# Seven block products for eight in the first product of a stacked graph network's layer 0

## The chip, the cores and the metric

The kernel runs on one core of a Trainium2 chip. The metric is device time in microseconds (us). The core works through its engines, each with its own queue of instructions: TensorE (PE in the profile) multiplies matrices, its weight loads are listed apart (PEld); VectorE (DVE), ScalarE (ACT) and GpSimd (POOL) work elementwise; SyncE (SP) issues most transfers. Before the change the kernel takes 2193.2 us, the median of three runs (2192.66 to 2193.32).

## The reference

Four graph layers are stacked over 128 graphs of 64 nodes with 256 features, all in float32, each followed by `x = layernorm(x + layer(x))`. Layer 0 is five small two-layer graph convolutions over groups of the first 25 nodes, weighted and summed:

```python
GROUPS = [list(range(25)), [0, 1, ..., 8], [0, 9, ..., 14], [6, 7, 8, 12, 13, 14], [3, 4, 5, 9, 10, 11]]

def _graph_conv(x, adj, W, b):
    A = adj + jnp.eye(n)
    ...                                  # dinv = rowsum(A) ** -0.5
    norm_adj = dinv[:, :, None] * A * dinv[:, None, :]
    support = jnp.einsum('bnd,de->bne', x, W)
    return relu(jnp.einsum('bnm,bme->bne', norm_adj, support) + b)

for g, idx in enumerate(GROUPS):
    h = _graph_conv(x[:, idx], adj[:, idx][:, :, idx], W1[g], b1[g])      # 256 -> 512
    out_g = _graph_conv(h, adj[:, idx][:, :, idx], W2[g], b2[g])          # 512 -> 256
    fused = fused.at[:, idx].add(softmax(fusion_w)[g] * out_g)
```

Layer 1 is a graph convolution over all 64 nodes, layer 2 a polynomial graph filter, and layer 3 five rounds of message passing with a GRU cell (products with `weight[l]`, `w_ih` and `w_hh`, of 256 and 768 outputs). Layer 3 is most of the work.

## The kernel before

Layer 0 goes through 16 units, numbered from 0. A unit takes up to four tiles of graphs of one group, and its columns are nodes. Groups come in the order 1, 2, 3, 4, 0, so units 0 to 2 belong to group 1 (504, 504 and 144 columns), 3 and 4 to group 2 (448 each), 5 and 6 to group 3 (504, 264), 7 and 8 to group 4 (504, 264), and 9 to 15 to group 0 (500 each, the last 200). For each unit the kernel gathers with the normalised adjacency (`aggregate`), multiplies by W1 (`hidden`), multiplies by W2 (`support`), gathers again (`add`) and, in group 0, normalises (`finish`):

```python
W1 = w0.tile([128, NG, 2, HID], F32, name="W1")      # all five groups' weights stay
W2 = w0.tile([128, NG, 4, D], F32, name="W2")
...
def aggregate(i):
    ...
    for k in range(2):
        p = psum0("pa0")
        for t, r in enumerate(u.rows):
            nc.tensor.matmul(p[:, u.off[t] : u.off[t] + r], xg[:r, t, k * 128 : (k + 1) * 128], AT[:r, t, :r], ...)
        with tc.high_priority():
            nc.scalar.copy(ag0[:, k, : u.cols], p[:, : u.cols])

def hidden(i):
    u = UNITS[i]
    ag0 = AG.pop(i)
    hg = keep.tile([128, 4, 512], F32, tag="NI", name="hg", bufs=2)
    for e in range(4):
        p = psum0("ph")[:, : u.cols]
        for k in range(2):
            nc.tensor.matmul(
                p, W1[:, u.g, k, e * 128 : (e + 1) * 128], ag0[:, k, : u.cols], start=k == 0, stop=k == 1
            )
        relus.append(
            nc.scalar.activation(hg[:, e, : u.cols], p, AF.Relu, bias=b1[:, u.g * 4 + e : u.g * 4 + e + 1])
        )
    HG[i] = hg

def support(i):
    ...
    for v in range(0, len(u.tiles), 2):
        p = psum0("ps").rearrange("p (t d) -> p t d", t=2)
        ts = range(v, min(v + 2, len(u.tiles)))
        for t in ts:
            for e in range(4):
                nc.tensor.matmul(
                    p[: u.rows[t], t - v, :], hg[:, e, u.off[t] : u.off[t] + u.rows[t]], W2[:, u.g, e, :],
                    start=e == 0, stop=e == 3,
                )
        ...                                          # copied to s2 on ScalarE
```

`prep` loads and normalises a unit's adjacency on DVE and POOL and transposes it on TensorE. The stages of neighbouring units are interleaved, and the order in which TensorE takes them is the order of this loop:

```python
for i in range(-2, NU + 1):
    if i >= 0:
        stage(load0, i + 3)
    stage(add, i - 1)
    if i:
        stage(aggregate, i + 1)
    early_stage(i, 0)
    stage(support, i)
    ...
    stage(finish, i - 1, g0)
    early_stage(i, 1)
    if i == -1:
        hidden(0)
        ...
    else:
        stage(prep, i + 2)
        stage(hidden, i + 1)
    if i == -2:
        load0(1, powers[0])
        load_second(1)
        load0(2, powers[0])
        load_first(2)
    elif i == -1:
        load_second(2)
        load_first(3)
    elif i == 0:
        load_second(3)
    elif i < 5:
        (load_first, load_second)[(i - 1) % 2]((4, 0)[(i - 1) // 2])
    early_stage(i, 2)
    for f, j in ((store_others, i - 1), (others, i), (load_others, i + 2)):
        ...            # the nodes outside the groups: load, layernorm, store
```

`load_first(g)` and `load_second(g)` load W1 and W2 of a group, each in one transfer of 512 KB. After layer 0 a `fold` multiplies the message weights of layer 3 with `w_ih`. Layer 3's products are already made by seven block products for eight: with both factors cut into 2x2 blocks, seven products of blocks and sums of blocks, added up rightly, give what eight block products give. The sums of weight blocks are `factors` (on DVE), those of data blocks `sums` (on POOL), and the additions of the products lie in the class `Gates` (copies on ACT, additions on DVE).

Of the kernel before, what the change touches and what calls it, by code (L numbers as in the profile page):

```python
# [68 lines left out]
def gnn_stack(  # L69
# [118 lines left out]

    def load_adj(c):
        a64 = keep.tile([128, NP, N], F32, name="a64", bufs=2)  # L190
        nc.sync.dma_start(a64, av[c])
        adjs[c] = a64
# [142 lines left out]
    with ExitStack() as c0:  # L335
        w0 = c0.enter_context(tc.tile_pool(name="w0", bufs=1))
        work = c0.enter_context(tc.tile_pool(name="work0", bufs=1))
        W1 = w0.tile([128, NG, 2, HID], F32, name="W1")
        W2 = w0.tile([128, NG, 4, D], F32, name="W2")
# [3 lines left out]
        loads, A, AG, HG, S2, Z, XO = {}, {}, {}, {}, {}, {}, {}  # L343
# [77 lines left out]
        def hidden(i):  # L421
            u = UNITS[i]
            ag0 = AG.pop(i)
            hg = keep.tile([128, 4, 512], F32, tag="NI", name="hg", bufs=2)
            for e in range(4):
                p = psum0("ph")[:, : u.cols]
                for k in range(2):
                    nc.tensor.matmul(  # L428
                        p, W1[:, u.g, k, e * 128 : (e + 1) * 128], ag0[:, k, : u.cols], start=k == 0, stop=k == 1
                    )  # L430
                relus.append(
                    nc.scalar.activation(hg[:, e, : u.cols], p, AF.Relu, bias=b1[:, u.g * 4 + e : u.g * 4 + e + 1])
                )
            HG[i] = hg

        def support(i):
            u = UNITS[i]
            hg, s2 = HG.pop(i), []
            for v in range(0, len(u.tiles), 2):
                p = psum0("ps").rearrange("p (t d) -> p t d", t=2)  # L440
                ts = range(v, min(v + 2, len(u.tiles)))
                for t in ts:
                    for e in range(4):
                        nc.tensor.matmul(  # L444
                            p[: u.rows[t], t - v, :], hg[:, e, u.off[t] : u.off[t] + u.rows[t]], W2[:, u.g, e, :],
                            start=e == 0, stop=e == 3,
                        )
                sv = work.tile([TR, 2, D], F32, name="s2", bufs=4)
                if u.rows[ts[0]] == u.rows[ts[-1]]:
                    nc.scalar.copy(sv[: u.rows[v], : len(ts), :], p[: u.rows[v], : len(ts), :])  # L450
                else:
                    for t in ts:
                        nc.scalar.copy(sv[: u.rows[t], t - v, :], p[: u.rows[t], t - v, :])
                s2 += [sv[:, t - v, :] for t in ts]
            S2[i] = s2
# [66 lines left out]
        def others(i):  # L522

            with tc.issue_after(evictions[-1].ins):
                layernorm(XO[i], n=XO[i].shape[1])

        def store_others(i):
            t = XO.pop(i)
            nc.sync.dma_start(xb[:, NP * i : NP * i + t.shape[1], :], t)
# [19 lines left out]
        def load_first(g):  # L549
            nc.sync.dma_start(W1[:, g], w1[g].rearrange("(k p) e -> p k e", p=128))  # L550

        def load_second(g):
            nc.sync.dma_start(W2[:, g], w2[g].rearrange("(k p) e -> p k e", p=128))

# [25 lines left out]
        g0 = next(i for i, u in enumerate(UNITS) if u.g == 0)  # L580
        for i in range(-2, NU + 1):
            if i >= 0:
                stage(load0, i + 3)
            stage(add, i - 1)
            if i:
                stage(aggregate, i + 1)
            early_stage(i, 0)
            stage(support, i)
            if not i:
                aggregate(1)  # L590
            if i == NU:
                folds = [products(0, q) for q in range(3)]
            stage(finish, i - 1, g0)
            early_stage(i, 1)
            if i == -1:

                hidden(0)
                with tc.issue_after(evictions[0].ins):
                    prep(1)
            else:  # L600
                stage(prep, i + 2)
                stage(hidden, i + 1)
            if i == -2:
                load0(1, powers[0])
                load_second(1)
                load0(2, powers[0])
                load_first(2)
            elif i == -1:
                load_second(2)
                load_first(3)  # L610
            elif i == 0:
                load_second(3)
            elif i < 5:
                (load_first, load_second)[(i - 1) % 2]((4, 0)[(i - 1) // 2])
# [58 lines left out]

# [4 lines left out]

    def factors(w):

        nc.vector.tensor_sub(w[:, :, 5, :], w[:, :, 4, :], w[:, :, 0, :])
        nc.vector.tensor_sub(w[:, :, 2, :], w[:, :, 1, :], w[:, :, 5, :])

    def fold():
# [7 lines left out]
        for l in range(L):  # L692
            for q in range(3):
# [10 lines left out]
                if q == 2:  # L704
                    factors(V[l])
                if q == 2 and l == 0:
                    nc.vector.tensor_add(WHH[:, :, 4, :], w21, WHH[:, :, 3, :])
                    nc.vector.tensor_sub(WHH[:, :, 6, :], WHH[:, :, 0, :], w21)
                    factors(WHH)
                yield  # L710

    def sums(a, name):

        t = work.tile([128, 4, H], F32, tag="T" + name, name="T" + name, bufs=2)
        nc.gpsimd.tensor_sub(t[:, 0:2, :], a[:, :, H:], a[:, 0, :].rearrange("p (s n) -> p s n", s=2))  # L715
        nc.gpsimd.tensor_sub(t[:, 2, :], a[:, 1, H:], t[:, 0, :])
        nc.gpsimd.tensor_sub(t[:, 3, :], a[:, 1, :H], t[:, 2, :])
        return t

    class Gates:  # L720

        def __init__(self, C, sides, name):
            self.C, self.sides, self.name = C, sides, name
            self.copies = {}

        def multiply(self, bank, i):
            for g, side in enumerate(self.sides):
                for m, (w, q, a, t) in enumerate(side):  # L730
                    rhs = {
                        1: a[:, 0, :H], 2: a[:, 1, :H], 3: a[:, 1, H:], 4: t[:, 3, :], 5: t[:, 0, :], 6: t[:, 2, :],
                        7: t[:, 1, :],
                    }[i]
                    nc.tensor.matmul(  # L735
                        bank[:, g, :], w[:, q, i - 1, :], rhs, start=i in (1, 2, 5) and g == 0 and m == 0,
                        stop=m == len(side) - 1, skip_group_check=True,
                    )

        def bank(self, s):  # L740
            return pg.tile([128, 2, H], F32, tag="pg", name=f"p{s}{self.name}")

        def product(self, i):
            C = self.C
            if i == 1:
                self.a = self.bank("a")
            if i in (1, 6, 7, 4):
                self.multiply(self.a, i)
                if i != 4:
                    c = self.copies[i] = work.tile([128, 2, H], F32, tag="copy", name=f"c{i}", bufs=4)  # L750
                    with tc.high_priority():
                        nc.scalar.copy(c, self.a)  # L752
                if i == 7:
                    nc.vector.tensor_add(C[:, :, 1, H:], self.d, self.copies.pop(7))  # L754
            elif i == 2:
                b = self.bank("b")
                self.multiply(b, i)
                nc.vector.tensor_add(C[:, :, 0, :H], b, self.copies.pop(1))  # L758
            else:
                if i == 5:  # L760
                    self.d = self.bank("d")
                self.multiply(self.d, i)
                if i == 3:
                    nc.vector.tensor_add(C[:, :, 0, H:], self.d, self.copies.pop(6))  # L764

    class Chunk:
# [12 lines left out]
        def state_of_layer2(self, k):  # L779
            if k:  # L780
                self.hT = work.tile([128, 2, NP * 128], F32, tag="hT", name="hT", bufs=4)
            p = self.transpose(lambda q, k: self.xt[:, q, k * 128 : (k + 1) * 128], k, "pT3")
            nc.scalar.copy(self.hT[:, k, :], p)
            if not k:
                self.th = sums(self.hT, "h")

        def messages(self, h=None):
            self.agg = gather(self.xt if h is None else h, self.A01, "agg", work, "agg", 2)
            self.ta = sums(self.agg, "a")

        def rz(self, i):
            if i == 1:
                self.RZ = keep.tile([128, 2, 2, NP * 128], F32, tag="RZ", name="RZ", bufs=2)
                self.g = Gates(
                    self.RZ, [[(WHH, q, self.hT, self.th), (V[self.l], q, self.agg, self.ta)] for q in (0, 1)], "rz"
                )
            self.g.product(i)
            RZ = self.RZ
            if self.last:
                self.last_rz(i)  # L800
                return
            for q in range(2):
# [8 lines left out]
        def n(self, i):  # L811
            if i == 1:
                self.NI = keep.tile([128, 2, 2, NP * 128], F32, tag="NI", name="NI", bufs=2)
                self.gn = Gates(
                    self.NI, [[(V[self.l], 2, self.agg, self.ta)], [(WHH, 2, self.hT, self.th)]], "n"
# [91 lines left out]
        def turn(self, k):  # L907
# [9 lines left out]
            if not last:  # L917
                with tc.high_priority():
                    nc.scalar.copy(self.h[:, :, f], pv)
                if not k:  # L920
                    self.th = sums(self.hT, "h")
# [175 lines left out]
```

## Time and profile before

| | before |
|---|---|
| median of three runs | 2193.2 us |
| profiled run | 2192.7 us |
| TensorE clock granted | 0.998 |
| ACT copies of layer 3's seven-product scheme, 128x512 (`c` L752) | 586 ns each |
| POOL 128x512 subtraction (`Ta` L715) | 1277 ns each |
| layer 0, fold, layer 3 | to 295 us, to 328 us, to the end |

The profile counts a float32 matmul as two records, so a group marked x16 is eight matmuls. A name such as `L428` is a line of the kernel: L428 is the matmul of `hidden`, L444 that of `support`, L413 and L466 those of `aggregate` and `add`, L399 the transposes of `prep`. A line of a timeline gives start and duration of a group of like instructions; because a group's last instruction overlaps the next group's first, the time that a group takes on TensorE is read from its start to the start of the next. A line of the waits gives total, number and longest wait in us. A line of groups gives busy time and mean length in ns, and then the idle time before it with what ended it.

### The profile page before, as it was taken

The page shows a single profiled execution, that of the slowest core. Times are in us where ns is not written, and L with a number is a line of the kernel's source. Part 1 is how long each engine was busy: PE and PEld are TensorE (multiplying, and loading weights), DVE is VectorE, ACT ScalarE, POOL GpSimd, SP SyncE. Part 2 cuts the span into 40 slices and gives each one's busy share as a digit, 9 for nine tenths or more (in the row PEclk, how much of TensorE's full clock was granted, in tenths as well). Part 3 has the DMA queues.
Part 4 walks back from the last instruction along what each step waited for, and adds up shares of the span by engine and source line. Part 5 has one row for each costly group of instructions (what it writes and reads, how often), then busy time and mean ns, then how long its engine had stood idle before and what let it go on. Part 6 is the DMA issues. An engine that isn't in the chain of part 4 may idle for free.

```text
span 2190.9 us, 30164 instructions
## 1 busy us (share of the span) xinstructions
PE 2176.9 (99%) x11542; PEld 1907.6 (87%) x11542; DVE 1363.6 (62%) x3067; ACT 1004.1 (46%) x1845; POOL 572.4 (26%) x621
## 2 busy tenths in 40 slices
PE   9999999999999999999999999999999999999998
PEld 6777888898988889888889898889898898888887
DVE  3445666566766666666766666657656666566556
ACT  3333334544544554444444454445444544455454
POOL 3211131222332222222322232232322222232222
PEclk9999999999999999999999999999999999999999
DMA  6532110000100010000000010001000000000000
GB/s 165 177 124 66 49 37 3 1 3 1 42 1 3 1 39 4 3 1 20 22 3 1 1 42 1 3 1 42 1 1 1 20 10 1 1 10 11 1 1 20
DMA packets 54204, 51.12 MB, mean 23 GB/s; under 512 B 20910, under 2 KB 49068, under 8 KB 54060
## 3 DMA queue, kind: packets, MB, share of 16 engines
q1 hardware_dynamic: 49552, 43.83, 6.6%
q0 software_dynamic: 1936, 4.83, 0.8%
q8 instruction: 91, 1.49, 0.3%
q10 hardware_dynamic: 2572, 0.54, 0.1%
q14 instruction: 53, 0.43, 0.1%
HBM read 32.40 MB, written 16.78 MB: 22 GB/s over the span
## 4 chain that ended last, share of the span: by engine, by line
PE 97%; DVE 2%; POOL 0%; issue 0%; ACT 0%; DMA 0%; ACTq 0%; POOLq 0%; DVEq 0%
PE parz L735 25%; PE pan L735 12%; PE pdrz L735 12%; PE pa L210 9%; PE pbrz L735 6%; PE pdn L735 6%; PE ps L444 4%; PE ph L428 4%; PE pT L776 4%; PE pbn L735 3%; PE pd L288 3%; PE pd L309 2%; PE pa L413 1%; PE po L466 1%; PE pf L562 1%; PE pp L278 1%
## 5 line engine op out<-in xcount | busy, mean ns | idle before, releaser
L752 ACT COPY c<-parz 128x512 f32<-128x512 f32 x240 | 140.7, 586 | 319.8 <-PE parz L735 319.2
L735 PE MATMUL parz<-Th,WHH 128*128 128x256 f32 x960 | 285.9, 379 | 0.2 <-ACT c L752 0.2
L735 PE MATMUL parz<-Ta,V 128*128 128x256 f32 x960 | 285.5, 379 | 0.0
L715 POOL TENSOR_TENSOR Th<-hn 128x512 f32<-128x512 f32 x64 | 81.6, 1275 | 777.6 <-DVE hn L840 602.9
L752 ACT COPY c<-pan 128x512 f32<-128x512 f32 x237 | 139.2, 587 | 149.5 <-PE pan L735 149.4
L837 ACT ACTIVATE NI<-NI,bih 128x512 f32<-128x512 f32 x158 | 113.9, 721 | 201.7 <-DVE NI L832 201.6
L735 PEld LDWEIGHTS parz<-Ta,V 128*128 128x128 f32 x960 | 182.4, 190 | 24.8
L735 PEld LDWEIGHTS parz<-Th,WHH 128*128 128x128 f32 x960 | 176.2, 190 | 21.3 <-ACT c L752 0.7
L809 ACT ACTIVATE RZ<-RZ,brz 128x512 f32<-128x512 f32 x158 | 114.6, 726 | 136.8 <-DVE RZ L764 136.8
L715 POOL TENSOR_TENSOR Ta<-agg 128x512 f32<-128x512 f32 x80 | 102.2, 1277 | 260.4 <-ACT agg L214 260.4
L764 DVE TENSOR_TENSOR RZ<-pdrz,c 128x512 f32<-128x512 f32 x80 | 55.0, 688 | 173.2 <-PE pdrz L735 173.2
L735 PE MATMUL pan<-Ta,V 128*128 128x256 f32 x474 | 141.2, 380 | 0.0
L735 PE MATMUL pan<-Th,WHH 128*128 128x256 f32 x474 | 141.0, 379 | 0.0
L139 POOL TENSOR_TENSOR rs<-ve,mhalf 128x4 f32<-128x4 f32 (+2 forms) x65 | 67.3, 1036 | 281.9 <-DVE ve L137 221.4
L758 DVE TENSOR_TENSOR NI<-pbn,c 128x512 f32<-128x512 f32 x79 | 54.7, 692 | 127.3 <-PE pbn L735 110.1
L210 PEld LDWEIGHTS pa<-A,h 128*128 128x128 f32 x1024 | 124.4, 192 | 3.3
L754 DVE TENSOR_TENSOR NI<-pdn,c 128x512 f32<-128x512 f32 x79 | 54.5, 690 | 112.8 <-ACT c L752 112.8
L210 PE MATMUL pa<-A,h 128*128 128x128 f32 x1024 | 124.6, 275 | 0.0
L838 DVE TENSOR_TENSOR RZ<-hn,NI 128x512 f32<-128x512 f32 x126 | 86.5, 687 | 48.5 <-ACT NI L837 48.5
L840 DVE TENSOR_TENSOR hn<-RZ,NI 128x512 f32<-128x512 f32 x158 | 108.4, 686 | 1.8
L839 DVE TENSOR_TENSOR RZ<-RZ 128x512 f32<-128x512 f32 x158 | 108.2, 685 | 1.8
L444 PE MATMUL ps<-W,hg 128*125 128x256 f32 (+5 forms) x464 | 103.6, 380 | 0.3 <-ACT v L315 0.3
(228 smaller groups left out, 5064.8 us busy)
## 6 DMA issues: line engine op xcount, KB each, us to landing
out_dram<-xt SPq DMA_DIRECT2D x30, 256.0 KB
W<-in_w_dram SPq DMA_DIRECT2D x10, 512.0 KB
xt<-xb SPq DMA_DIRECT2D x32, 156.0 KB
xo<-in_x_dram SPq DMA_DIRECT2D x9, 512.0 KB
xb<-xo SPq DMA_DIRECT2D x9, 512.0 KB
xt<-xa SPq DMA_DIRECT2D x32, 100.0 KB
xg<-in_x_dram SPq DMA_DIRECT2D x25, 125.0 KB
xa<-xg SPq DMA_DIRECT2D x25, 125.0 KB
```

Of the source, the lines that this page charges most:

```text
L210: nc.tensor.matmul(p[:, q * 128 : (q + 1) * 128], src[:, q, k * 128 : (k + 1) * 128], m[:, q, :], start=True, stop=True)
L428: nc.tensor.matmul(p, W1[:, u.g, k, e * 128 : (e + 1) * 128], ag0[:, k, : u.cols], start=k == 0, stop=k == 1)
L444: nc.tensor.matmul(p[: u.rows[t], t - v, :], hg[:, e, u.off[t] : u.off[t] + u.rows[t]], W2[:, u.g, e, :], start=e == 0, stop=e == 3,)
L715: nc.gpsimd.tensor_sub(t[:, 0:2, :], a[:, :, H:], a[:, 0, :].rearrange("p (s n) -> p s n", s=2))
L735: nc.tensor.matmul(bank[:, g, :], w[:, q, i - 1, :], rhs, start=i in (1, 2, 5) and g == 0 and m == 0, stop=m == len(side) - 1, skip_group_ ...
L752: nc.scalar.copy(c, self.a)
L776: nc.tensor.transpose(p[:, q * 128 : (q + 1) * 128], src(q, k), ident)
L809: nc.scalar.activation(RZ[:, q, 0, :], RZ[:, q, 0, :], AF.Sigmoid, bias=b[0])
L837: nc.scalar.activation(n, n, AF.Tanh, bias=bih[:, 4 + j : 5 + j])
L838: e.tensor_sub(d, self.hT[:, j, f], n)
L839: e.tensor_mul(d, d, z)
L840: e.tensor_add(self.hn[:, j, f], d, n)
```

## The change

In the large units among units 4 to 11, `hidden` makes its product of 256x512 weights with the aggregated columns by seven block products instead of eight. The 512 outputs are two sides of 256; for each side the 256x256 weight block is cut into 2x2 blocks, and the columns of the unit into two halves. So a unit's eight matmuls of full width become fourteen of half width. The purpose is to take work from TensorE. `hidden` becomes a generator, and the loop spreads its products between the other stages so that copies and additions can lie beside TensorE's other work. W1 and W2 no longer stay resident: they go through rings of two and three buffers, W1 is laid out as the seven blocks that the scheme needs, comes in four transfers of 128 KB, and is loaded later. The normalisation of the nodes outside the groups is held back by one stage, and in the fold, the block sums of the later rounds' weights come behind the fold's products. The functions `factors`, `sums` and the class `Gates` are moved up to be shared; the parts of them that stay alike are cut here.

```diff
+    def factors(w, w21=None):
+        if w21 is not None:
+            nc.vector.tensor_add(w[:, :, 4, :], w21, w[:, :, 3, :])
+            nc.vector.tensor_sub(w[:, :, 6, :], w[:, :, 0, :], w21)
+        nc.vector.tensor_sub(w[:, :, 5, :], w[:, :, 4, :], w[:, :, 0, :])
+        nc.vector.tensor_sub(w[:, :, 2, :], w[:, :, 1, :], w[:, :, 5, :])
...
+        def product(self, i):
+            C, h = self.C, self.h
+            if i == 1:
+                self.a = self.bank("a")
+            if i in (1, 6, 7, 4):
+                self.multiply(self.a, i)
+                if i != 4:
+                    c = self.pool.tile([128, 2, H], F32, tag="copy", name=f"c{i}", bufs=4)[:, :, :h]
+                    self.copies[i] = c
+                    with tc.high_priority():
+                        nc.scalar.copy(c, self.a)
+                if i == 7:
+                    nc.vector.tensor_add(C[:, :, 1, h:], self.d, self.copies.pop(7))
+            elif i == 2:
+                b = self.bank("b")
+                self.multiply(b, i)
+                nc.vector.tensor_add(C[:, :, 0, :h], b, self.copies.pop(1))
+            else:
+                if i == 5:
+                    self.d = self.bank("d")
+                self.multiply(self.d, i)
+                if i == 3:
+                    nc.vector.tensor_add(C[:, :, 0, h:], self.d, self.copies.pop(6))
...
-        W1 = w0.tile([128, NG, 2, HID], F32, name="W1")
-        W2 = w0.tile([128, NG, 4, D], F32, name="W2")
...
-        def hidden(i):
+        def hidden(i, seven=True):
...
+            if not seven or u.cols < 400:
+                for _ in range(5):
+                    yield
+                ...                                   # eight matmuls, as before
+                return
+            h = u.cols // 2
+            with tc.high_priority():
+                t = sums(ag0, work, "0", 1)
+            C = hg.rearrange("p (g j) n -> p g j n", g=2)[:, :, :, : u.cols]
+            taken[0] += 1
+            g7 = Gates(C, [[(w, g, ag0, t)] for g in range(2)], work, lambda s: psum0("ph" + s))
+            for m in (1, 6, 2, 5, 7, 4, 3):
+                yield
+                with tc.high_priority():
+                    g7.product(m)
+                for g in range(2):
+                    j, f = {2: (0, slice(0, h)), 7: (1, slice(h, 2 * h)), 3: (0, slice(h, 2 * h))}.get(m, (1, slice(0, h)))
+                    if m in (2, 7, 3, 4):
+                        nc.scalar.activation(C[:, g, j, f], C[:, g, j, f] if m != 4 else g7.a[:, g, :], AF.Relu, bias=b(2 * g + j))
...
         def others(i):
             with tc.issue_after(evictions[-1].ins):
-                layernorm(XO[i], n=XO[i].shape[1])
+                NO[i] = norm_stats(XO[i], n=XO[i].shape[1])
+                if i >= 8:
+                    norm_apply(XO[i], *NO.pop(i), n=XO[i].shape[1])
         def store_others(i):
             t = XO.pop(i)
+            if i in NO:
+                with tc.issue_after(evictions[-1].ins):
+                    norm_apply(t, *NO.pop(i), n=t.shape[1])
...
         def load_first(g):
-            nc.sync.dma_start(W1[:, g], w1[g].rearrange("(k p) e -> p k e", p=128))
+            W1[g] = w0.tile([128, 2, 7, 128], F32, tag="W1", name=f"W1{g}", bufs=2)
+            W21[g] = w0.tile([128, 2, 128], F32, tag="W21", name=f"W21{g}", bufs=2)
+            v = w1[g].rearrange("(k p) (q e) -> p k q e", p=128, q=2)
+            for k in range(2):
+                nc.sync.dma_start(W1[g][:, :, k, :], v[:, k, :, :128])
+            nc.sync.dma_start(W21[g], v[:, 0, :, 128:])
+            nc.sync.dma_start(W1[g][:, :, 3, :], v[:, 1, :, 128:])
...
             stage(add, i - 1)
+            next(cur, None)
             if i:
                 stage(aggregate, i + 1)
+            for _ in cur:
+                pass
             early_stage(i, 0)
-            stage(support, i)
+            nxt = hidden(i + 1, 2 < i < g0 + 2) if 0 <= i + 1 < NU else iter(())
+            if 0 <= i < NU:
+                for last in support(i):
+                    if last and i:
+                        next(nxt, None)
+                        next(nxt, None)
...
                 stage(prep, i + 2)
-                stage(hidden, i + 1)
+                for _ in range(3):
+                    next(nxt, None)
+            next(nxt, None)
+            cur = nxt
...
-                load_first(3)
...
-            elif i < 5:
-                (load_first, load_second)[(i - 1) % 2]((4, 0)[(i - 1) // 2])
+            elif i in (2, 4, 6):
+                g = {2: 3, 4: 4, 6: 0}[i]
+                load_first(g)
+                if i == 2:
+                    with tc.issue_after(evictions[-1].ins), tc.issue_after(powers[-1].ins):
+                        factors(W1[2], W21[2])
+            elif i in (3, 5, 7):
+                g = {3: 3, 5: 4, 7: 0}[i]
+                if i < 7:
+                    load_second({3: 4, 5: 0}[i])
+                with tc.issue_after(evictions[-1].ins), tc.issue_after(powers[-1].ins):
+                    factors(W1[g], W21[g])
...
-                if q == 2:
+                if q == 2 and l == 0:
                     factors(V[l])
-                if q == 2 and l == 0:
...
-                    factors(WHH)
+                if q == 2 and l == 1:
+                    factors(WHH, w21)
                 yield
...
+        for w in V[1:]:
+            factors(w)
```

## The prediction

> **What bounds the kernel now.** I read the header and the busy shares first, then the chain that ended last, then the waits of the matmul engine, and then its timeline over layer 0, which the change touches. From the page:
>
> ```profile
> span 2190.9 us, 30164 instructions
> PE 2176.9 (99%) x11542; PEld 1907.6 (87%) x11542; DVE 1363.6 (62%) x3067; ACT 1004.1 (46%) x1845; POOL 572.4 (26%) x621
> PE 97%; DVE 2%; POOL 0%; issue 0%; ACT 0%; DMA 0%; ACTq 0%; POOLq 0%; DVEq 0%
> ```
>
> TensorE is busy for 99% of the span, and 97% of the chain is its own work. There is next to no wait to remove. The time can fall only where TensorE does less, and it rises by whatever wait comes new. The chain by lines gives `ph L428` 4% of the span: this is layer 0's first product, all that is attacked, and only in some of its units.
>
> All the waits of TensorE in layer 0 and the fold (0 to 330 us):
>
> ```profile
> PE pw L536 <- DVE zero L533: 1.5, 1, 1.5
> PE pT L776 <- DVE V L703: 0.9, 1, 0.9
> PE pa L413 <- DVE AT L403: 0.8, 1, 0.8
> PE pT L399 <- DVE A L391: 0.3, 1, 0.3
> PE ps L444 <- ACT v L315: 0.3, 1, 0.3
> ```
>
> That is 3.8 us in five places. So every us that TensorE saves in layer 0 comes off the end, if its partners keep up. Its timeline (start, duration; a record pair is one matmul, so x16 is eight):
>
> ```profile
> 72.31 6.18 PE L428 MATMUL ph<-ag,W 128*128 128x448 f32 x16
> 78.33 1.94 PE L466 MATMUL po<-AT,s 112*128 112x112 f32 x16
> ...
> 81.90 7.07 PE L444 MATMUL ps<-W,hg 128*112 128x256 f32 x32
> 88.81 0.48 PE L399 MATMUL pT<-ident,A 126*126 126x126 f32 x3
> 89.23 7.03 PE L428 MATMUL ph<-ag,W 128*128 128x504 f32 x16
> 96.09 1.94 PE L466 MATMUL po<-AT,s 112*128 112x112 f32 x16
> ...
> 107.13 3.73 PE L428 MATMUL ph<-ag,W 128*128 128x264 f32 x16
> 110.69 1.95 PE L466 MATMUL po<-AT,s 126*128 126x126 f32 x16
> ```
>
> Start to next start, eight matmuls of 448 columns take 78.33 - 72.31 = 6.02 us, of 504 columns 96.09 - 89.23 = 6.86 us (0.8575 each), of 264 columns 3.56 us (0.445 each). The sixteen of 256 columns in `ps` take 88.81 - 81.90 = 6.91 us (0.432 each). Units of 500 columns take 6.71 us (151.19 to 157.90).
>
> [...] the slope between 256 and 504 columns is (0.8575 - 0.4317)/248 = 1.717 ns a column, which leaves a fixed part of about zero. [...] here a 128x512 one takes 1277 ns on POOL (`Ta` L715) and 688 on DVE (`RZ` L764). [...] the changed loads of W1 have exactly 512-byte rows. No more than that: in the trace a 512-byte packet takes 27 ns and a 2048-byte one 84, so four times 27 against 84 is 1.3 times the transfer time.
>
> **Saved.** The loop switches to seven products for units 4 to 11 where a unit has 400 columns or more. I count units 4 (448), 5 and 7 (504), 9, 10 and 11 (500): six, one more than the title says. In each, 8 full-width matmuls become 7 products x 2 halves of the weight = 14 of half width.
> - 504: half is 252 columns, 0.4317 - 4 x 0.0017 = 0.425 us; 14 x 0.425 = 5.95; saved 6.86 - 5.95 = 0.91, twice: 1.82.
> - 500: 250 columns, 0.421; 5.90; saved 6.71 - 5.90 = 0.81, three times: 2.43.
> - 448: 224 columns, 0.377; 5.28; saved 0.74.
> Sum 5.0 us, 0.23% of the span. The eighth of `ph` that one expects is 0.125 x 40.7 = 5.1; the same number by another way.
>
> **Added beside TensorE.** For each such unit: three subtractions on POOL (1.28 + 0.73 + 0.73 = 2.75 us), three copies on ACT (about 0.58 each, as `c` L752 of the same size), eight half-width relus (about 0.48 as at 264 columns, 3.8 us) for four (0.68, 2.7 us), three additions on DVE (0.69 each). For each of four weight groups four DVE factor operations (about 0.42, 1.7 us). A unit's stage is some 18 us; ACT was busy 19.2 us of the 50 from 50 to 100 us, DVE 23.3, POOL 13.1. Each takes on 2 to 4 us more in a stage of 18, and none comes near full. Totals are not the danger; order is.
>
> **What these could make TensorE wait for.** The products are spread out: 1 in the middle of `support`; 6, 2, 5, 7 after the adjacency transposes; 4 after the next `add`; 3 after the next `aggregate`. Between a bank's product and the next that overwrites it:
> - Products 1, 6, 7 and 4 accumulate in one bank, and each copy must be out before the next product. Between 1 and 6 stand at least four matmuls of `support` (1.7 us) and the transposes (0.4); from 6 to 7 stand 2 and 5 (1.7 us) against a copy of 0.6 and its start. From 7 to 3 stand `add`, 4 and `aggregate` (1.9 + 0.85 + 1.9 = 4.6 us) against a copy and an addition (1.3).
> - The sums: needed by product 6, which comes a `support` (7 us) after `aggregate`'s copy; 2.75 us on POOL.
> - Relus: product 3 closes just before `support`; its addition and two relus are 0.7 + 1.0 us, and the output is needed after the part of `support` ahead of it. The half of rows that only products 1 and 2 make comes first, so the tile that needs product 3 comes about 4 us later.
> All have slack, but some only about 1 us, with semaphores and the in-order queues of ACT and DVE in between. I put 0.5 us on all of them together, an estimate.
>
> **Moved.** (1) W1 comes in four pieces of 128 KB instead of one of 512 KB. An issue costs the SP queue 0.4 to 0.7 us, so at the start the three extra pieces push back the adjacency of unit 1. DVE waited for it until 15.28 us, and TensorE took its transposes at 19.2 with some 0.8 us of slack. Estimated wait: 0.3 us. (2) The weights lie in rings, so W1 of groups 3, 4 and 0 comes at stages 2, 4 and 6 instead of at once, and DVE makes the factors when they land. DVE is in order: if the load is late, everything behind it stands. Group 3 lands, I estimate, near 69 us and is needed at 72.5; group 0 near 131 and needed at 135. Group 4 is tight. Its pieces are issued behind the eight `xg` loads that are in the queue at 105.6:
>
> ```profile
> 105.03 0.47 SPq L519 DMA_DIRECT2D xo<-in_x_dram  x1
> 105.61 8.21 SPq L364 DMA_DIRECT2D xg<-in_x_dram  x8
> 113.86 2.29 SPq L191 DMA_DIRECT2D a<-in_adj_dram  x2
> ```
>
> Loads issued in this stretch landed 6 to 8 us later. I get the last pieces issued at about 106 to 108 and landed at 110 to 112. DVE reaches the factors right after its transpose eviction at 107.3. Behind them are the factors themselves (1.7), the delayed normalisation (1.4), the statistics (1.75) and the power round trip of the next adjacency (3.4): 8.4 us to the transposes of unit 8, which TensorE takes at about 119.3. So 112 + 8.4 is 1 us late, 110 + 8.4 is in time, and a landing at 117, as the worst of these loads, is 6 us late. I put 0.3 to 0.5 on it, with a tail. (3) The factors of the later rounds' `V` go behind the fold. The wait there (0.9 us on `V` L703) ends with DVE, which just before is at the last layer normalisation; the order of DVE up to that point stays as it is, so I leave this wait as it was.
>
> **Sum.** -5.0 (products) + 0.5 (chains) + 0.3 (start) + 0.4 (late weights) = -3.8, so 2193.2 - 3.8 = 2189.4; I say 2189.2.
>
> **Rivals.** (a) DVE is blocked behind a late weight load. For: in order, and the estimate is in time by nothing. Against: SP's queue is freed by the group-3 and group-0 loads that no longer stand early. It would give 3 to 7 us back: 2192 to 2197. (b) The chains of seven products do not close: 0.5 to 1 us of wait in each of six units, and the gain is gone: 2192 to 2194. For: copies and relus sit behind each other on ACT. Against: the GRU rounds, which use the same scheme with the same copies, show 0.2 us of wait in 240 copies. (c) All hidden: 2193.2 - 5.0 = 2188.2. (d) All hidden, and the fold's wait goes too: 2187.3.
>
> **Range and chances.** (c) and what I sum to are the bulk; (a) and (b) make the long upper side. 2187.3 to 2193.2 should hold it 8 times in 10. For 2% it would take 44 us, more than half of all of `ph` (4% of the span) on the gaining side, and a broken prefetch in several stages on the other.
>
> **What would show it.** In the profile after, `ph` of the large units should stand as groups of 252, 250 and 224 columns at 0.425, 0.421 and 0.377 us of spacing; TensorE's busy time should fall by about 5.0 us; its waits in layer 0 should be the five of before and no more than about 1.5 us beside. A `pT` of unit 8 that waits on DVE with a `W1` load ahead of it is (a). Waits of `ph` on ACT or DVE are (b). I am wrong if half-width matmuls show a fixed cost (0.02 us on each of 84 is 1.7 us), or if the whole of layer 0 slides for a load.

## The result and the profile after

The changed kernel takes 2205.8 us (median of four runs, 2202.8 to 2206.1) where the kernel before takes 2193.3 in the same comparison. The ratio is 1.0054 with a 95% interval of 1.0037 to 1.0071: slower by 0.5%, 12.6 us, where a gain of 4 us was forecast.

The header, busy shares and chain of the page after:

```profile
span 2204.3 us, 30432 instructions
PE 2179.5 (99%) x11614; PEld 1926.0 (87%) x11614; DVE 1387.4 (63%) x3101; ACT 1016.1 (46%) x1887; POOL 588.6 (27%) x639
PE 95%; DVE 3%; POOL 1%; DMA 0%; issue 0%; ACT 0%; POOLq 0%; SPq 0%; DVEq 0%; ACTq 0%
```

TensorE's busy time should have fallen by 5 us and rose by 2.6; and its share of the chain fell from 97% to 95%. So there are two things to find: waits, and work that takes longer. The waits of TensorE (total, number, longest):

```profile
PE pf L662 <- DVE V L826: 3.7, 1, 3.7
PE pT L467 <- DVE d0o L125: 3.2, 1, 3.2
PE pT L467 <- DVE A L459: 3.2, 2, 2.3
```

These are new, 10.1 us: one in the fold (`pf`), three at adjacency transposes (`pT`); the others in the list are those of before. None is a wait of a product for its copies or additions. The timeline of TensorE in unit 5, where nothing waits, and around the two places in layer 0 (start, duration; at the end of a line the idle time before it and what ended it):

```profile
90.80 1.01 PE L224 MATMUL phb<-ag,W 128*128 128x252 f32 x4
91.65 1.01 PE L224 MATMUL phd<-T,W 128*128 128x252 f32 x4
...
122.75 0.41 PE L467 MATMUL pT<-ident,A 126*126 126x126 f32 x2 [3.23 <-DVE d0o L125]
124.12 0.18 PE L467 MATMUL pT<-ident,A 12*12 12x12 f32 x1 [0.96 <-DVE A L459]
124.23 2.05 PE L224 MATMUL pha<-T,W 128*128 128x252 f32 x4
126.08 1.89 PE L224 MATMUL phb<-ag,W 128*128 128x252 f32 x4
127.76 1.89 PE L224 MATMUL phd<-T,W 128*128 128x252 f32 x4
...
194.02 0.67 PE L467 MATMUL pT<-ident,A 125*125 125x125 f32 x4 [2.26 <-DVE A L459]
194.53 1.47 PE L224 MATMUL pha<-T,W 128*128 128x250 f32 x4
195.79 1.88 PE L224 MATMUL phb<-ag,W 128*128 128x250 f32 x4
```

The first wait is at unit 8's transposes, between unit 7's products 1 and 6; the second at unit 12's, between unit 11's. Behind each the same product takes twice its time: two matmuls of 252 columns take 127.76 - 126.08 = 1.68 us. In unit 5 they take 91.65 - 90.80 = 0.85, as forecast. The busy time of the engines in three stretches of 20 us (busy us, and the granted clock in the third column from the right) gives the reason:

```profile
core 0: us, PE busy (x) PEld busy (x) DVE busy (x) ACT busy (x) POOL busy (x), PEclk, DMA share, GB/s
116.00:136.00 20.00, 15.80 (x67) 11.97 (x67) 14.31 (x61) 6.96 (x15) 7.47 (x8) 0.83 0.56 173
186.00:206.00 20.00, 17.74 (x99) 15.86 (x98) 16.23 (x50) 9.03 (x18) 5.74 (x6) 0.91 0.20 62
320.00:340.00 20.00, 16.32 (x82) 14.18 (x81) 11.41 (x26) 5.94 (x18) 11.88 (x12) 0.91 0.07 20
```

TensorE's clock was halved. A mean of 0.83 over 20 us is 20 x 0.17 x 2 = 6.8 us at half clock; 0.91 is 3.4 to 3.6 us. Each us at half clock in which TensorE works loses half a us (1.68 us for a product of 0.85). In the kernel before the mean from 60 to 330 us is 1.00.

The ledger of the two profiled runs. Up to `support` of the last unit (290.57 us before, 297.62 after, so +7.05): products -4.6 (as the best kernel below has it), waits 3.2 + 1.0 + 2.3, half clock (6.8 - 0.9 + 3.4)/2 = 4.7, for 0.9 us of it fell into the second wait, where nothing is lost, and +0.5 ahead of the first `support` (20.11 for 19.63 us); sum +7.1. The fold (38.07 us before, 43.37 after, +5.3): wait 3.7 and half clock (3.4 - 0.6)/2 = 1.4. The rest of layer 3 is 1.05 us longer, which I did not trace; it lies between 1862.3 and 1863.6 us in all the kernels below, and repairs in layer 0 don't sort it.

**Why unit 8 waited.** DVE and the SP queue, timelines of the kernel after:

```profile
106.29 0.68 DVE L471 TENSOR_TENSOR AT<-pT,d0o 126x504 f32<-126x504 f32 x1 [6.49 <-PE pT L467]
113.22 0.42 DVE L193 TENSOR_TENSOR W<-W,W 128x256 f32<-128x256 f32 x1 [6.24 <-DMA W<-in_w_dram]
...
120.56 2.05 DVE L459 TENSOR_TENSOR A<-ae,block 126x126 f32<-126x126 f32 x2
```

```profile
102.86 1.15 SPq L432 DMA_DIRECT2D xg<-in_x_dram  x1
107.94 0.33 SPq L607 DMA_DIRECT2D xo<-in_x_dram  x1
108.37 1.25 SPq L647 DMA_DIRECT2D W<-in_w_dram  x2
109.67 0.60 SPq L649 DMA_DIRECT2D W<-in_w_dram  x1
```

DVE stood 6.24 us at the first factor operation for W1 of group 4. Its last pieces were issued from 108.37 on, because the `xo` load ahead of them stood in the queue from 104.0 to 107.94, until the store `xb` that frees its buffer had landed (at 107.9); they landed at 113.2. From there it took 122.75 - 113.22 = 9.5 us to the transposes, for which I had 8.4.

**Why unit 12 waited.** The same two DVE operations of layer 1's preparation, first in the kernel before, then after, and then POOL in the kernel after:

```profile
174.63 0.66 DVE L227 TENSOR_TENSOR Ab<-a,pair 128x512 f32<-128x512 f32 x1
176.40 1.06 DVE L154 TENSOR_SCALAR xo<-xo,mv,rs 128x256 f32<-128x256 f32 x3 [0.71 <-POOL rs L139]
```

```profile
183.39 1.56 DVE L295 TENSOR_TENSOR Ab<-a,pair 128x512 f32<-128x512 f32 x1
185.99 1.83 DVE L154 TENSOR_SCALAR xo<-xo,mv,rs 128x256 f32<-128x256 f32 x3
```

```profile
183.04 1.36 POOL L202 TENSOR_TENSOR T<-ag 128x500 f32<-128x500 f32 x1 [2.23 <-ACT ag L486]
185.92 0.63 POOL L203 TENSOR_TENSOR T<-ag,T 128x250 f32<-128x250 f32 x1
```

From unit 11's `AT` to unit 12's `A`, DVE took 14.8 us before (169.15 to 183.99) and 19.35 after (174.53 to 193.88): three additions (2.0 us), a third normalisation of outer nodes (1.4, held back from the stage before into one that had two already), and 0.9 + 0.8 us by which `Ab` and `xo` are longer. Both of these overlap POOL's sums; in the kernel before, POOL does nothing beside either (idle from 173.2 to 175.51 us and from 176.36 to 179.07). TensorE before reached the transposes 3.0 us after they were ready; now 2.3 us too soon. That POOL's sums make the 0.9 + 0.8 us is my reading of the overlap; an experiment below (the sums on DVE) bears on it.

**Why the fold waited.** POOL's queue, in the kernel before and then after:

```profile
304.00 1.07 POOL L139 TENSOR_TENSOR rs<-ve,mhalf 125x1 f32<-125x1 f32 x2 [3.15 <-DVE ve L137]
305.04 0.79 POOL L687 DMA_DIRECT2D wh<-in_whhT_dram  x1
```

```profile
311.04 1.07 POOL L139 TENSOR_TENSOR rs<-ve,mhalf 125x1 f32<-125x1 f32 x2 [3.15 <-DVE ve L137]
316.72 0.80 POOL L810 DMA_DIRECT2D wh<-in_whhT_dram  x1 [4.60 <-DVE V L826]
```

The load of `wh21`, and with it the three of `WHH` behind it, goes out 4.6 us later. The page's releaser (`V`) is only the last of what it waited for: POOL's semaphore waits ahead of the load end one by one at 314.60, 315.76 and 315.99 us, where the last `xa` stores of layer 0 landed (314.57, 315.74, 315.96). DVE then stands 4.1 us at the factors of `WHH`, and the evictions of the fold's products stand behind it.

### The profile page after: what moved, and what is told of

It is laid out like the page before. It is cut to its first block, busy times and chain, and to the rows that moved or that the text cites. A ratio compares the mean times of both kernels' runs of the same rounds, so it can differ in the third digit from the quotient of the medians.

```text
span 2204.3 us, 30432 instructions
## 1 busy us (share of the span) xinstructions
PE 2179.5 (99%) x11614; PEld 1926.0 (87%) x11614; DVE 1387.4 (63%) x3101; ACT 1016.1 (46%) x1887; POOL 588.6 (27%) x639
## 4 chain that ended last, share of the span: by engine, by line
PE 95%; DVE 3%; POOL 1%; DMA 0%; issue 0%; ACT 0%; POOLq 0%; SPq 0%; DVEq 0%; ACTq 0%
PE parz L224 25%; PE pan L224 12%; PE pdrz L224 12%; PE pa L278 9%; PE pbrz L224 6%; PE pdn L224 6%; PE ps L532 4%; PE pT L848 4%; PE pbn L224 3%; PE pd L356 3%; PE pd L377 2%; PE ph L504 2%; PE pa L481 1%; PE po L554 1%; PE pha L224 1%; PE pp L346 1%
```

## The experiments

The theory from these readings: the products give what was forecast; the loss is three separate waits beside them, each with half-clock time behind it. The main rival: the seven products themselves cost, or DVE is too full as a whole, so that a wait that is removed comes back further on. "Before" is 2193.1 to 2193.3 us in all comparisons. Where the expectations speak of the wait at unit 11, they mean the one at unit 12's transposes, between unit 11's products.

**W1 of group 4 earlier.** The load keeps its place in the program; the loads that had gone ahead of it come behind.

```diff
-                stage(load0, i + 3)
+                if i in (6, 7):
+                    load0(i + 3, late[3])          # late[3]: the last piece of W1 of group 4
+                else:
+                    stage(load0, i + 3)
...
-                        f(o)
+                        with tc.issue_after(late[3].ins) if f is load_others and i in (5, 6, 7) else nullcontext():
+                            f(o)
```

> The changed kernel, with one thing moved: the three late pieces of W1 of group 4 come before the x loads of units 9 and 10 and before the next load of the outer nodes. Theory (three separate waits, each with a half-clock window behind it): the wait at unit 8's transposes goes (3.2 + 1.0 us) and with it 6.8 us at half clock, worth 3.4; so 2205.8 - 7.6 = about 2198, and the waits at unit 11 and in the fold stay. Rival (DVE is too full as a whole): the wait comes back at the next stage, and the time falls by less than 3 us, to 2203 or more.

Measured: 2198.6 us (2196.1 to 2199.2), 7.2 less. Both waits at unit 8 and the half clock there are gone (unit 7's products take 122.02 - 121.17 = 0.85 us behind the transposes); the wait at unit 12 (2.2) and that of the fold (3.6) stay as they were, though in this trace the fold's products stay slow for longer: the eight behind the wait take 3.55 and 2.35 us in two fours, against 3.18 and 1.73 in the changed kernel. The theory holds here and the rival doesn't.

**The tile wh21 in another place.** One allocation is moved up, behind `WHH`; no instruction changes its place.

```diff
     WHH = work.tile([128, 3, 7, 128], F32, name="WHH")
+    w21 = work.tile([128, 3, 128], F32, name="wh21")
     V = [work.tile([128, 3, 7, 128], F32, name=f"V{l}") for l in range(L)]
...
     def fold():
-        w21 = work.tile([128, 3, 128], F32, name="wh21")
```

> The changed kernel, with the tile wh21 of the fold allocated right behind WHH instead of behind the five V, so that it does not lie on memory that the last stores of layer 0 still read; nothing else. Theory: the loads of w_hh go out some 5 us sooner, DVE isn't held by them, the 3.7 us wait of the fold's products goes and the 3.4 us half-clock window behind it (1.7 us): 2205.8 - 5.4 = about 2200.4. Rival (the fold's wait comes from the factors that stand in DVE's queue, not from the load): 2205 to 2206.

Measured: 2200.0 us (2197.9 to 2200.6), 5.8 less. POOL issues the load at 310.1, straight behind its `rs`; the fold's wait is 0.5 us and there is no half clock behind it (1.00 from 316 to 336 us). Between the two traces lie 6.6 us, of which the fold has 4.5 (38.83 for 43.37); most of the rest is the half clock at unit 8, 3.4 us here (0.91 from 114 to 134 us) for 6.8, which the edit does not touch. So the fold's loss is a matter of which memory a tile got: by what its load waited for, `wh21`, allocated last, lay on buffers that the last stores still read. That the new sizes of layer 0's pools put it there is inferred; the traces have no addresses.

**Five units.** `2 < i < g0 + 1` for `g0 + 2`.

> The changed kernel with eight products in unit 11 (five seven-product units, as the title counts). Theory: the wait at unit 11's transposes (2.3 us) and the half-clock window behind it (1.7) go, the saving of one unit (0.8) is lost: 2205.8 - 3.2 = about 2202.6. Rival (each seven-product unit costs time by itself): about the same step for each unit, so some 2 us, and the wait of 2.3 us is still in the list, at unit 10 or 12.

Measured: 2202.3 us (2201.7 to 2203.2), the time that was expected, but only partly for its reason. The wait at unit 12 is 1.3 us and not gone, though no half clock follows it (the eight matmuls behind it take 197.04 - 190.33 = 6.71 us, as units of 500 columns did before). Unit 8's first wait is 2.3 us for 3.2, and the half clock behind it 3.4 us for 6.8, which the edit does not touch: over 20 us at unit 8 the mean clock is 0.83 in the changed kernel, and 0.91 here and with `wh21` moved. Half of the 3.4 us between them gives, as an estimate, an uncertainty of about 2 us for one time of a kernel with such waits.

**Eight products everywhere.** `hidden(i + 1, False)`: all that is beside the products stays, their additions go.

> The changed kernel with eight products in every unit: weight rings, later loads, factors on DVE, held-back normalisation and the new fold all stay. Theory: what is beside the products costs the fold's 5.4 us and about 1 us of wait at unit 8, for DVE still stands behind W1 of group 4, but TensorE comes later: 2199 to 2200. Rival (the products themselves bring the loss): 2193 to 2194.

Measured: 2199.3 us (2197.3 to 2200.9). The fold's wait (3.5 us) and its half clock are there (the first four products behind it take 324.24 - 321.67 = 2.57 us, for 1.73 at full clock), 5.4 us in the fold; unit 8 did not wait, where about 1 us was expected. So what lies beside the products costs some 6 us without any saving, and the wait at unit 8 takes both: the late load, and a TensorE that comes earlier with a DVE that has additions to do.

**Both repairs with five, six and no units.** The two edits above together; with five units; with six and one constant changed; with eight products everywhere.

```diff
-                if i >= 8:
+                if i >= 7:
                     norm_apply(XO[i], *NO.pop(i), n=XO[i].shape[1])
```

> W1 of group 4 early, wh21 behind WHH, and five seven-product units (eight products in unit 11). Theory: no wait at unit 8, 0.5 us in the fold, the wait at unit 12's transposes of about 1.3 us that stood with five units, no half-clock window: 2193.2 - 4.2 + 1.3 + 0.6 = about 2191. Rival (removed waits come back elsewhere): 2194 or more.

> W1 of group 4 early, wh21 behind WHH, all six units, and the normalisation of the outer nodes done at once from the eighth block on (i >= 7 for i >= 8), so that DVE doesn't have three of them in the stage before unit 12's transposes. Theory: DVE has 1.4 us less to do there, the wait falls from 2.3 to 0.9 us and is too short for a half-clock window: 2193.2 - 5.0 + 0.9 + 0.6 = about 2189.7. Rival (DVE there is held by POOL's sums and not by its amount of work): wait and window stay, 2192.5.

> W1 of group 4 early, wh21 behind WHH, eight products in every unit: all of the change that lies beside the products, with the two repairs. Theory: only 0.2 us at the start and 0.5 us in the fold are left, 2193.9; with the five-unit kernel of the same call this gives the products' own worth, 4.2 us less what DVE costs. Rival (rings, later loads and factors cost more than the waits tell): 2195 or more.

Measured: 2191.7 us (2190.9 to 2192.2) with five; 2189.6 (2188.9 to 2190.5) with six and the constant; 2194.1 (2193.7 to 2196.0) with none. With six units, header, busy shares and the waits at the two places that are left:

```profile
span 2187.1 us, 30427 instructions
PE 2172.3 (99%) x11614; PEld 1921.4 (88%) x11614; DVE 1385.6 (63%) x3101; ACT 1015.6 (46%) x1887; POOL 587.8 (27%) x639
```

```profile
PE pT L467 <- DVE A L459: 0.5, 1, 0.5
PE pf L664 <- DVE V L832: 0.4, 1, 0.4
```

TensorE's busy time is 4.6 us below before, and the clock is full from 60 to 330 us (1.00). From none to six the time falls by 2194.1 - 2189.6 = 4.5 us; with the 0.5 us of wait at unit 12 added back that is 5.0. The traces have a little less: from the first unit's `support` to the last one's, 270.94 us before and 266.83 with six, and with the wait added back 4.6 saved. So the products are worth 4.6 to 5.0 us, for 5.0 forecast. (The constant differs too between none and six; it acts through the wait, and the last experiment changes it further without effect.) What is left beside it is 0.8 us (2194.1 against 2193.3), most of it in the fold and not clear of the noise (ratio 0.9995 to 1.0012). The six-unit kernel beats both: ratio to before 0.9984, interval 0.9977 to 0.9990. The wait at unit 12 fell from 2.2 to 0.5 us, a little more than the 1.4 us of normalisation that was moved.

**Idle filled.** The changed kernel, unrepaired, with matmuls of no use where TensorE would wait:

```diff
             p = psum0("pT").rearrange("p (t n) -> p t n", t=4)
+            for _ in range({8: 14, 12: 10}.get(i, 0)):
+                nc.tensor.matmul(p[:, 0, :], ident, ident, start=True, stop=True)
```

> The changed kernel with idle filled: 14 matmuls of the identity with itself (0.217 us each, 3.0 us) ahead of unit 8's transposes and 10 (2.2 us) ahead of unit 12's, into the bank that the transposes then overwrite. It adds work and takes no wait away. Theory (the half clock follows from idle time): TensorE is as late as before but keeps its full clock; 2 or 3 windows of 3.4 us at half clock vanish, 3.4 to 5.1 us, so about 2201 to 2202.5; the fold's stays. Rival (the slow matmuls behind the waits have another cause, such as the late data): 2205 to 2206.

Measured: 2203.5 us (2201.0 to 2204.9), 2.3 less, a little short of the range. The four times overlap those of the changed kernel (2202.8 to 2206.1), so it is the trace that decides. Its timeline at unit 8, and the busy time and clock of the three stretches:

```profile
118.94 3.39 PE L444 MATMUL pT<-ident 128*128 128x128 f32 x28
122.40 0.44 PE L469 MATMUL pT<-ident,A 126*126 126x126 f32 x2
...
124.91 1.01 PE L224 MATMUL phb<-ag,W 128*128 128x252 f32 x4
125.76 1.01 PE L224 MATMUL phd<-T,W 128*128 128x252 f32 x4
```

```profile
116.00:136.00 20.00, 18.91 (x107) 15.42 (x106) 15.46 (x64) 7.90 (x17) 7.47 (x8) 1.00 0.55 174
186.00:206.00 20.00, 18.66 (x119) 16.81 (x118) 13.62 (x40) 8.41 (x18) 4.41 (x4) 1.00 0.30 93
320.00:340.00 20.00, 16.40 (x80) 14.12 (x79) 11.09 (x30) 5.86 (x19) 8.85 (x9) 0.91 0.01 2
```

The transposes come as late as in the changed kernel (122.40 against 122.75), but the products behind them run at 0.85 us a pair and the clock is 1.00; the fold, where nothing was filled, still has 0.91. So in layer 0 the half clock came with the idle time (15.80 and 17.74 us busy of 20 in the changed kernel, 18.91 and 18.66 here) and not with the late data. Behind unit 12's transposes, after unit 11's product 7, this kernel is 4.9 us ahead of the unfilled one (194.67 against 199.59), of which 0.5 were there before the first filler (117.11 against 117.62). Up to the last unit's `support` 3.1 us of it are left (294.52 against 297.62): product 4 then waits 1.3 us for a copy on ACT that stood behind a relu, a wait that is not in the list of the unfilled kernel.

**The sums on DVE.** In the best kernel, the three subtractions of the data blocks go to DVE.

```diff
-                t = sums(ag0, work, "0", 1)
+                t = sums(ag0, work, "0", 1, nc.vector)
```

> The kernel with both repairs and norm at once from the eighth block, with the three subtractions of the data blocks on DVE for POOL. Theory (POOL's two-input subtractions hold up DVE instructions that overlap them): DVE gets 1.5 us more work a unit, but the three normalisations that took 2.28 us beside POOL's sum take 1.06 us; the time stays within 1 us of 2189.6. Rival (these normalisations are stretched by something else): they still take 2 us or more, DVE has 1.5 us more to do in unit 12's stage, and its wait of 0.5 us grows to 2 us: 2191 or more.

Measured: 2190.1 us (median; lowest 2189.4). The normalisation of three blocks of outer nodes in unit 11's stage, first in the best kernel, with the sum on POOL that it meets, then with sums on DVE:

```profile
174.87 1.22 POOL L202 TENSOR_TENSOR T<-ag 128x500 f32<-128x500 f32 x1 [0.24 <-ACT ag L486]
174.67 2.28 DVE L154 TENSOR_SCALAR xo<-xo,mv,rs 128x256 f32<-128x256 f32 x3 [0.74 <-POOL rs L139]
```

```profile
175.03 1.06 DVE L154 TENSOR_SCALAR xo<-xo,mv,rs 128x256 f32<-128x256 f32 x3 [0.74 <-POOL rs L139]
```

The theory holds: with the sums off POOL the three take 1.06 us for 2.28, 1.2 us less of DVE's time in this stage, and none of the seven normalisations from 160 to 190 us takes more than 0.413. It isn't worth moving the sums: DVE then does them itself (0.67 + 0.41 + 0.41 us), and the wait at unit 12 is 0.5 us either way.

**Nine units, and the normalisation at once.** Seven products in units 12 to 14 too (`g0 + 5`); and, apart from it, the outer nodes never held back (`i >= 0`).

> The kernel with both repairs and norm at once from the eighth block, with seven products in units 12, 13 and 14 too (nine units). Theory: TensorE saves 0.81 us in each, 2.4 us, but DVE is busy for 11 to 15 of each 20 us there, and gets three additions and the collisions with POOL's sums on top: waits of DVE take most of it, 2188 to 2191. Rival (the scheme is free wherever no load is late): 2187.2 and no new wait.

> The kernel with both repairs and all six units, with the outer nodes' normalisation never held back, as in the kernel before. Theory: DVE waits about 0.8 us for POOL in each of eight stages again, and each normalisation comes between the transposes' eviction and the next adjacency; only where a stage is tight does it show: within 1 us of 2189.6. Rival (holding it back is needed to have room for the additions): a wait of over 1 us in the early units, 2191 or more.

Measured: 2190.1 and 2189.9 us (medians). In the nine-unit kernel two new waits appear, and the one in the fold grows to 0.7:

```profile
PE po L554 <- DVE xt L361: 1.4, 1, 1.4
PE pa L481 <- ACT v L383: 1.0, 1, 1.0
```

They take the 2.4 us that three more units save. Where group 0 runs beside layers 1 and 2, DVE and ACT had no room for more at these two places. Holding the normalisation back is not needed: without it, and with both repairs, the time is the same within a few tenths of a us.

## Why the prediction was wrong

**Saved: right.** 5.0 us forecast, 4.6 to 5.0 shown. The half-width matmuls cost 0.425 (252 columns), 0.42 (250) and 0.38 us (224), and no fixed part shows among like products: two of 250 columns take 0.84 us, one of 500 took 0.839. In the units of 504 columns a product behind another kind of work takes some 0.1 us more (89.84 to 90.80 and 97.80 to 98.75 in the changed kernel, 0.95 for 0.85), so these units save about 0.1 us less each. The check by another way used 40.7 us for `ph`; the six times above it add to 39.9, an eighth of which is 5.0.

**Chains of seven products: right, and even too careful.** 0.5 us was put on them; no wait for a copy or an addition of layer 0's products stands in the lists of the changed and of the best kernel, so rival (b) falls. The slack is thin, though: with idle filled, one such wait of 1.3 us appeared.

**Moved, (1), the start:** 0.3 us forecast, as a wait at unit 1's transposes; the list after has none there. The changed kernel's trace comes to its first `support` 0.5 us later (20.11 for 19.63), but the traces of the experiments, with the same loads, come to it between 19.1 and 20.0. A cost at the start is not shown.

**Moved, (2), the late load: the mechanism was named and its size missed.** "I put 0.3 to 0.5 on it, with a tail" is the first step that failed, and rival (a), given as "3 to 7 us", is what happened: 4.2 us of wait. The landing came at 113.2 for "110 to 112", since I had put W1 behind the eight `xg` loads, and it stood behind an `xo` load that held the queue for 3.9 us until a store had landed; and the chain behind it took 9.5 us for 8.4 (the four parts named for it add to 8.25), part of it in DVE's two `A`, which took 2.05 us beside POOL's sum (121.22 to 122.46 us) for 0.49 in the kernel before. A sum that ends "in time by nothing" is worth its tail, not its median.

**What a wait costs: missing from every term.** I took a wait of 3 us as 3 us, with a price for a matmul and none for a wait. In the changed kernel the waits of 3.2 + 1.0 us at unit 8, 2.3 at unit 12 and 3.7 in the fold brought 6.8, 3.4 and 3.4 us at half clock, so 3.0, 1.7 and 1.4 us on top: 4.7 us in layer 0 and 1.4 in the fold, 6.1 of the 13.4 us between the two traces.

**Added beside TensorE: "Totals are not the danger; order is"** failed for the stage before unit 12. An average slack over a stage of 18 us was the wrong measure: this stage carries layer 1's preparation as well, DVE had 3.0 us to spare there, and got 4.5 us more.

**Moved, (3), the fold:** "I leave this wait as it was" rested on the order of DVE, which is indeed the same up to that point. The order of instructions says nothing of when a load may start. The moved allocation shows that a tile's memory decides it: a wait of 3.7 us became 0.5, and the fold 4.5 us shorter. I had no term for it, and no rival.

**Range:** all three misses lie on one side, and the upper end stood at one late load without a clock behind it.

## What to carry to other kernels

On a TensorE that is busy all the time (99% of the span here), a saving shortens the time only where every stage's partners have more slack than the saving plus what the saving adds to them; read the slack at each stage's releasing operation, not as a busy share. Price a wait at its length plus the clock that is lost behind it: the waits of 2.3, 3.7 and 3.2 + 1.0 us here lost 1.7, 1.4 and 3.0 us more, while one of 1.3 us (five units) lost none. The two at unit 8 cost some 7 us, more than all the products brought. When pools change size, look at what each early load of the next phase then has to wait for.

## What the runs showed of the hardware

**Waits and the clock.** In the changed kernel TensorE's granted clock is at half from 123.26 to 130.09 us, from 194.94 to 198.35, from 328.06 to 331.47 and from 2195.15 to the end. From one change to the next it is 6.83, 64.85, 3.41, 129.71, 3.41 and 1863.7 us, which is 2, 19, 1, 38, 1 and 546 times 3.413. In the kernel before it falls to half once, at 2182.86. The stretches of 3.41 us on both sides of these changes, and one with a wait in it and full clock on both sides:

| kernel, stretch (us) | TensorE idle in it (us) | clock in it | clock in the next |
|---|---|---|---|
| after, 119.85 to 123.26 | 3.00 | 1.00 | 0.50 |
| after, 123.26 to 126.67 | 0.86 | 0.50 | 0.50 |
| after, 126.67 to 130.09 | 0.00 | 0.50 | 1.00 |
| after, 191.53 to 194.94 | 2.26 | 1.00 | 0.50 |
| after, 194.94 to 198.35 | 0.00 | 0.50 | 1.00 |
| after, 310.99 to 314.40 | 0.89 | 1.00 | 1.00 |
| after, 324.65 to 328.06 | 3.07 | 1.00 | 0.50 |
| after, 328.06 to 331.47 | 0.61 | 0.50 | 1.00 |
| after, 2191.73 to 2195.15 | 2.31 | 1.00 | 0.50 |
| before, 2179.45 to 2182.86 | 2.31 | 1.00 | 0.50 |

More than these cases the two traces do not show. The idle time of the last row is made of two waits, of which neither alone is over 1.55 us:

```profile
2181.50 0.44 PE L882 MATMUL pT<-ident,hn 128*128 128x128 f32 x2 [1.55 <-DVE hn L872]
2182.69 0.57 PE L882 MATMUL pT<-ident,hn 128*128 128x128 f32 x2 [0.76 <-DVE hn L872]
```

Waits of like length did not always bring the same: at unit 8 the kernel with `wh21` moved waited 3.1 + 1.0 us, nearly as the changed kernel did (3.2 + 1.0), and had 3.4 us at half clock for 6.8. What decided between them is not shown.

**DVE beside POOL.** In the changed kernel three normalisations of 128x256 took 1.83 us beside POOL's two 128x250 subtractions, the longest 0.88 us; in the kernel before three took 1.06 us, none over 0.413. `Ab` (128x512) took 1.56 us beside a 128x500 subtraction for 0.66, and two elementwise multiplications of 126x126 took 2.05 us beside one of 128x504 for 0.49. In the kernel with both repairs and six units three normalisations took 2.28 us, and 1.06 with the sums on DVE.
